# Value projection of token tiles 1 to 7 computed between the steps of an iterative pseudo-inverse and kept in device memory

## The chip, the cores and the metric

The kernel runs on one core of a Trainium2 chip. The metric is the device time of one execution in microseconds (us), and the time of a kernel is the median of its runs. The profile is one further execution of the same program, taken with the hardware profiler. TensorE appears in it as PE (matmuls) and PEld (weight loads), VectorE as DVE, ScalarE as ACT, GpSimd as POOL; SP is the engine that issues most of the plain transfers, in order.

## The reference, cut to what matters

Two layers follow one another. The first is a Nyström attention with a graph gate; its result `xo` replaces the tokens, and a mixture of experts works on these. With `dense` the layer-normed input of 4 x 1024 tokens of width 256, all in float32:

```
attn2_inv = pinv(attn2)            # 6 iterations on 8 matrices of 64 x 64
    xz = x @ z;  z = 0.25 * z @ (13*I - xz @ (15*I - xz @ (7*I - xz)))
xg    = attention of batch 0 (attn1 @ (attn2_inv @ (attn3 @ v)) + conv, output projection)
enc   = xg[0] + dense
A_raw = segment_sum(adj_vals * scores[adj_rows, adj_cols]);  alpha = softmax(A_raw)
value = dense @ wv_w + wv_b        # the value projection of this case: 256 x 256 weights
xl    = alpha[:, None] * value
sw    = sigmoid(-xl) ** 2
xo    = xl * 2 * sw + 2 * enc * (1 - sw)
```

`value` needs only the normed input and two weights. It needs neither the attention nor `alpha`. After this each token goes to expert 0 and to one of seven others (gated silu networks, width 1024).

## The kernel before, in words

The 4096 tokens are cut into 8 token tiles: tile `t` holds tokens 128t to 128t+127 of each of the 4 batches, as `x[t]`, 128 partitions by 4 x 256. All of `x` stays on the chip. The work has these stages:

- 0 to 60 us: inputs, layer-norm statistics `stats[t]` of all tiles (so that a normed tile is one ScalarE pass per batch), `d0T` (the normed batch 0 of all tiles, already transposed), landmarks and weights of the attention.
- 60 to 121 us: the pseudo-inverse. `prod` (L827 to 833) multiplies 8 pairs of 64 x 64 matrices into a PSUM tile; lines 848 to 864 loop over 6 iterations of four such products (`psq`, `pza`, `pzu`, `pzT`; the last iteration has no `pza`), each followed by small VectorE or ScalarE steps (`zu`, `sq`, `zy`, `za`, `zw`, `zT`) on which the next product waits. VectorE works at the same time on the edge lists (`picks`: L253 and L254), and POOL writes the edges to memory with indirect transfers (L276, 73 of them).
- 121 to 187 us: the attention's scores and softmaxes (`score`, `soft`; L917, L926, L934, L947), in pieces. The score tiles use the same two PSUM buffers (`pz`) as the pseudo-inverse.
- 187 to 283 us: output of the attention, the gate `alpha` from the edges, tile 0.
- 283 to 661 us: the dense expert on 8 tiles. The loop issues for each tile `t`: `up(t)` for two of eight column blocks, `down(t-1)`, `prologue(t+1)`, and the other six blocks of `up(t)`. In `up` (L1433) each block takes the PSUM buffers `pa` and `pb` out of four; ScalarE's silu (`sa`, L1444) frees the one, VectorE's product (`h`, L1446) the other.
- 661 to 1063 us: the seven routed experts, in 13 pairs and some single slots of 128 rows.

`prologue(t)` (L1304) normalizes tile `t` (L462), makes its value projection (`turned`, L510: 8 transposes into two PSUM tiles `ptv`, copied to `tv` by VectorE and ScalarE; `values`, L519: 8 products of 128 x 256 with `wv_sb`, and the bias at L534), adds the attention (`added`, L469 and L472), mixes (`mixed`: sigmoid L484, square L488, then L485, L491, L492, statistics, transposes L503), routes the tokens (L1321 to L1354) and writes their slots to memory with POOL (`place`, L1299). `place` reuses its small tile `info` after two tiles, so that VectorE's writes of the next one (L1294) wait for POOL's transfers.

A float32 product shows as two matmul rows and two weight-load rows in the profile, a transpose as one of each.

The order of the work on each engine is made when the program is built: instructions are laid out by expected readiness, per engine, and run in that order. Buffers are taken out of pools in the order of the source. Lines that the change touches: the pseudo-inverse loop (L848 to 864) and lines 1309 to 1312 in `prologue`.

Of the kernel before, what the change touches and what calls it, by code (L numbers as in the profile page):

```python
# [7 lines left out]
F32 = mybir.dt.float32  # L8
BF16 = mybir.dt.bfloat16
I32 = mybir.dt.int32  # L10
AF = mybir.ActivationFunctionType
ALU = mybir.AluOpType
# [4 lines left out]
P = 128  # L17
B, N, D = 4, 1024, 256
NT = N // P
KD = D // P  # L20
# [28 lines left out]
def tile_kernel(  # L49
# [20 lines left out]
    nc = tc.nc  # L70
    mm = nc.tensor.matmul

    def pool(name, bufs=1, **kw):
        return tc.tile_pool(name=name, bufs=bufs, **kw)
# [3 lines left out]
    dram = ctx.enter_context(pool("dram", space=DRAM))  # L78
# [7 lines left out]
    x = [xa[:, t] for t in range(NT)]  # L86
# [26 lines left out]
    ident = const.tile([P, P], F32, name="ident")  # L113
# [47 lines left out]

    meta_d = dram.tile([ROWS, 4], F32, name="meta_d")
    conv_d = dram.tile([H, P * (CW + 1)], F32, name="conv_d")

# [290 lines left out]
    val = [None] * NT  # L457
# [52 lines left out]
    def turned(tt, xt, name, ps, tag, on=None):  # L510

        for k in range(KD):
            pt = ps.tile([P, B, P], F32, tag=tag, name=f"ptv{name}_{k}")
            for b in range(B):
                nc.tensor.transpose(pt[:, b, :], xt[:, b, k * P : (k + 1) * P], ident)
            evac(k if on is None else on, tt[:, k], pt)
        return tt

    def values(t, tt, ps, tag):  # L519

        vt = late.tile([P, B, D], F32, tag="T", name=f"val{t}")
        val[t] = vt
        pvs = []
        for b2 in range(2):
            pv = ps.tile([P, 2, D], F32, tag=tag, name=f"pval{t}_{b2}")
            pvs.append(pv)
            for i in range(2):
                for k in range(KD):
                    mm(pv[:, i, :], lhsT=tt[:, k, 2 * b2 + i, :], rhs=wv_sb[:, k, :],
                       start=(k == 0), stop=(k == KD - 1))  # L530

        def bias():
            for b2 in range(2):
                nc.vector.tensor_tensor(  # L534
                    vt[:, 2 * b2 : 2 * b2 + 2, :], pvs[b2],
                    wvb.unsqueeze(1).to_broadcast([P, 2, D]), ALU.add
                )
        return bias


    with ExitStack() as at:
        wp = at.enter_context(pool("aw"))
        ps = at.enter_context(pool("aps", 4, space=PSUM))
# [14 lines left out]
        for a in a_v:  # L558
            for half in range(2):
                nc.sync.dma_start(  # L560
                    out=a[:, :, half * 512 : half * 512 + 512],
                    in_=zero.unsqueeze(1).to_broadcast([P, NT, 512]),
# [3 lines left out]
        d0T = wp.tile([P, KD, N], F32, name="d0T")  # L566
# [10 lines left out]
        wv_sb = const.tile([P, KD, D], F32, name="wv_sb")  # L577
        nc.sync.dma_start(out=wv_sb, in_=wv_w.rearrange("(k p) d -> p k d", p=P))
        wvb = const.tile([P, D], F32, name="wvb")
# [7 lines left out]
            out=conv_d.rearrange("h (p x) -> p h x", x=CW + 1),  # L587
            in_=zero[:, 0 : CW + 1].unsqueeze(1).to_broadcast([P, H, CW + 1]),
        )
        nc.sync.dma_start(  # L590
            out=conv_d.rearrange("h (p x) -> p h x", x=CW + 1)[:, :, 0:CK],
            in_=conv_rev.unsqueeze(0).to_broadcast([P, H, CK]),
        )
        nc.sync.dma_start(
            out=band, in_=conv_d[:, 0 : P * CW].rearrange("h (p j) -> p h j", j=CW)
# [37 lines left out]
        for i in range(2):  # L633
            wt = ap.tile([P, NP, D], F32, name=f"wT{i}", bufs=1)
            wT.append(wt)
            for h2 in range(2):
                pt = ps.tile([P, 2, D], F32, tag="ps", name=f"ptw{i}_{h2}")
# [13 lines left out]
        stats = [(rstda[:, t], nmra[:, t]) for t in range(NT)]  # L651
        for b in range(B):
# [4 lines left out]
            rstd, nmr = rstda[:, :, b], nmra[:, :, b]  # L657
# [10 lines left out]
            for i, a in ((i, a) for i in range(4) for a in range(2)):  # L668
                t = 4 * a + i
                mm(pool_x[32 * a : 32 * a + 32, b, :], lhsT=gw[:, a, i], rhs=x[t][:, b, :],  # L670
                   start=(i == 0 and b % 2 == 0), stop=(i == 3 and b % 2 == 1))
        for t in range(NT):
            a, i = divmod(t, 4)
            mm(pool_m[32 * a : 32 * a + 32], lhsT=near[:, i], rhs=nmra[:, t, :],
               start=(i == 0), stop=(i == 3))
        for t in range(NT):
# [4 lines left out]
            pt = ps.tile([P, 512], F32, tag="ps", name=f"ptr{t}")[:, 0 : KD * P].rearrange(  # L681
                "p (k n) -> p k n", k=KD
            )
# [7 lines left out]
        pt = ps.tile([P, KD, B, M], F32, tag="ps", name="ptl")  # L691
# [35 lines left out]
        for c in range(NP):  # L727
            pl = ps.tile([P, 2, B * M], F32, tag="ps", name=f"pl{c}")
            for i in range(2):
                f0 = i * H * DH + c * P  # L730
                for k in range(KD):
                    mm(pl[:, i, :], lhsT=wqk8[:, k, f0 : f0 + P],
                       rhs=pT[:, k].rearrange("p b m -> p (b m)"),
                       start=(k == 0), stop=(k == KD - 1))
# [10 lines left out]
        for h2 in range(2):  # L745
            pa2 = ps.tile([P, 8, M], F32, tag="ps", name=f"pa2_{h2}")
            for i in range(8):
                b, c = divmod(h2 * 8 + i, NP)
# [69 lines left out]
        vp = conv.enter_context(pool("v"))  # L818
        inv = ExitStack()
        zp = inv.enter_context(pool("inv", 2))  # L820

        def zt(tag, name):
            return zp.tile([P, NP, M], F32, tag=tag, name=name, bufs=2 if tag in ("za", "zT") else 1)

        def prod(name, lhsT, rhs):  # L827
            pz = psz.tile([P, 2, NP, M], F32, tag="pz", name=name)[:, 0]
            for c in range(NP):
                for j in range(2):  # L830
                    r = slice(64 * j, 64 * j + 64)
                    mm(pz[r, c, :], lhsT=lhsT[r, c, :], rhs=rhs[r, c, :], start=True, stop=True)
            return pz
# [12 lines left out]
        stt = nc.vector.scalar_tensor_tensor  # L846
        for it in range(PINV):
            psq = prod(f"psq{it}", za, za)  # L848
            zu = zt("zu", f"zu{it}")
            stt(zu, za, 7.0, psq, ALU.mult, ALU.subtract)  # L850
            if it < PINV - 1:
                sq = zt("sq", f"sq{it}")
                nc.scalar.activation(sq, psq, AF.Copy, scale=0.25)
                zy = zt("zy", f"zy{it}")
                stt(zy, za, 13.0 / 15.0, psq, ALU.mult, ALU.subtract)
                pza = prod(f"pza{it}", sq, zu)
                zn = zt("za", f"za_{it + 1}")
                stt(zn, zy, 3.75, pza, ALU.mult, ALU.add)
            zw = zt("zw", f"zw{it}")
            stt(zw, za, -15.0, id13.unsqueeze(1).to_broadcast([P, NP, M]), ALU.mult, ALU.add)  # L860
            nc.vector.tensor_tensor(zw, zw, prod(f"pzu{it}", za, zu), ALU.add)
            zTn = zt("zT", f"zT_{it + 1}")
            nc.scalar.activation(zTn, prod(f"pzT{it}", zw, zT), AF.Copy, scale=0.25)
            za, zT = zn, zTn


        tok = const.tile([P, NT * B], F32, name="tok")
# [436 lines left out]
    def prologue(t):  # L1304
        if t:
            def tile_(what):
                return tp.tile([P, B, D], F32, tag=what, name=f"{what}{t}", bufs=2)

            enc = tile_("enc")
            normed(enc, t)  # L1310
            tt = tp.tile([P, KD, B, P], F32, tag="tt", name=f"tv{t}", bufs=1)
            values(t, turned(tt, enc, t, pm, "pm"), pm, "pm")()
            added(enc, t)
            mixed(t, enc, tile_, pm, "pm")
        yt = yT[t]


        pl = pm.tile([P, 512], F32, tag="pm", name=f"plt{t}")
        for k in range(KD):
            for b in range(B):  # L1320
                mm(pl[32 * b : 32 * b + 32, 0:P], lhsT=wr_sb[:, k, :], rhs=yt[:, k, b, :],  # L1321
                   start=(k == 0), stop=(k == KD - 1))
        lg = tp.tile([P, P], F32, tag="lg", name=f"lg{t}", bufs=1)
        nc.scalar.copy(lg, pl[:, 0:P])
        nc.tensor.transpose(pl[:, P : 2 * P], lg, ident)
        plg = pl[:, P : 2 * P].rearrange("p (b e) -> p b e", b=B)[:, :, 0:NX]

        def small(name, w):
            return tp.tile([P, B, w], F32, tag=name, name=f"{name}{t}")

        def bc(a, w):
            return a.to_broadcast([P, B, w])

        mx, sm = small("gmx", 1), small("gsm", 1)
        p, eq, best = small("gp", NX), small("geq", NX - 1), small("gbest", 1)
        den = small("gden", 1)
        nc.vector.tensor_reduce(mx[:, :, 0], plg, AX.X, ALU.max)
        nc.vector.tensor_tensor(p, plg, bc(mx, NX), ALU.subtract)
        nc.scalar.activation(p, p, AF.Exp)
        nc.vector.tensor_reduce(sm[:, :, 0], p, AX.X, ALU.add)  # L1340
        nc.vector.reciprocal(sm, sm)
        nc.vector.tensor_tensor(p, p, bc(sm, NX), ALU.mult)
        nc.vector.tensor_reduce(mx[:, :, 0], p[:, :, 1:NX], AX.X, ALU.max)
        nc.vector.tensor_tensor(eq, p[:, :, 1:NX], bc(mx, NX - 1), ALU.is_equal)
        nc.vector.tensor_tensor(eq, eq, desc.unsqueeze(1).to_broadcast([P, B, NX - 1]), ALU.mult)
        nc.vector.tensor_reduce(best[:, :, 0], eq, AX.X, ALU.max)
        nc.vector.tensor_tensor(eq, eq, bc(best, NX - 1), ALU.is_equal)
        nc.vector.tensor_tensor(den, p[:, :, 0:1], mx, ALU.add)
        nc.vector.tensor_scalar_max(den, den, 1e-9)
        nc.vector.reciprocal(den, den)  # L1350
        nc.vector.tensor_tensor(mx, mx, den, ALU.mult)
        g = main.tile([P, B, 1], F32, tag="gates", name=f"gates{t}")
        gates[t] = g
        nc.vector.tensor_tensor(g, p[:, :, 0:1], den, ALU.mult)  # L1354
        place(t, eq, mx)
# [347 lines left out]
```

## Time and profile before

| what | value |
|---|---|
| runs of the kernel before | 1073.0, 1072.16, 1064.18 us; median 1072.16 us |
| the profiled execution's own time | 1065.04 us |
| its span, first to last instruction | 1063.3 us, mean granted TensorE clock 0.967 |
| busy: PE, PEld, DVE, ACT, POOL | 989.2, 685.7, 437.6, 303.6, 226.2 us |
| stage of the pseudo-inverse, 64.5 to 121.1 us | PE busy 38.4, DVE 29.6, ACT 9.8 of 56.6 us; clock 0.83 |
| one period of the dense expert, 421 to 469 us | PE busy 48.0, DVE 21.9, ACT 20.8 of 48.0 us; clock 1.00 |

How to read it: the busy share of PE over the whole span (93%) mixes a first quarter, in which PE often waits, with the experts, in which it does not. What a change is worth has to be read stage by stage. Busy times count instructions by their modelled ends; for matmuls the distance from one start to the next is the better measure of what one costs.

### The profile page before, as it was taken

Reading aid. Unit: us, or ns where it says so; the run is one execution under the profiler, and the core shown is the slowest. Engines: PE = TensorE matmul, PEld = TensorE weight load, DVE = VectorE, ACT = ScalarE, POOL = GpSimd, SP = SyncE. Lnnn points to the kernel's source line nnn. Section 1 sums busy time; section 2 is a strip of 40 time slices with the busy share of each in tenths; the row PEclk is TensorE's granted clock in tenths of the full one; section 3 lists DMA queues with packets and bytes.
Section 4 is the critical chain, followed back from the end, with each engine's and each line's share of the span. In section 5 each row is a group of like instructions: output and inputs, shape, how many; then the busy total and the mean of one; then the engine's idle time right before and its main releaser. Section 6 shows DMA issues by size and latency. Waiting matters only on the chain. (4 is left out here: it accounts for less than half of the span.)

```text
span 1063.3 us, 13557 instructions
## 1 busy us (share of the span) xinstructions
PE 989.2 (93%) x5042; PEld 685.7 (64%) x5042; DVE 437.6 (41%) x1262; ACT 303.6 (29%) x605; POOL 226.2 (21%) x236
## 2 busy tenths in 40 slices
PE   3867787988999999999999999999999999999996
PEld 2744345564647475756657466888888888866664
DVE  8875477476763544535363621112121211222221
ACT  5321354130661625435171600111101111111111
POOL 1246663003011001010101020332223222322111
PEclk9898897989999999999999999999999999999998
DMA  9810000532300000001010052556545554578880
GB/s 341 290 36 2 1 2 2 218 110 12 140 21 21 20 20 21 20 21 39 1 40 21 21 163 80 178 180 204 206 148 182 208 204 149 189 278 317 297 290 20
DMA packets 74473, 125.30 MB, mean 118 GB/s; under 512 B 11645, under 2 KB 51966, under 8 KB 74400
## 3 DMA queue, kind: packets, MB, share of 16 engines
q1 hardware_dynamic: 63808, 108.50, 29.6%
q0 software_dynamic: 8848, 14.14, 4.5%
q10 hardware_dynamic: 1744, 1.70, 0.5%
q8 instruction: 43, 0.70, 0.3%
q14 instruction: 30, 0.25, 0.1%
HBM read 101.86 MB, written 23.13 MB: 118 GB/s over the span
## 5 line engine op out<-in xcount | busy, mean ns | idle before, releaser
L1441 PE MATMUL pa<-yT,w_a 128*128 128x512 f32 x256 | 124.3, 595 | 0.2 <-issue 0.2
L1441 PE MATMUL pb<-yT,w_a 128*128 128x512 f32 x256 | 122.3, 595 | 0.0
L1453 PE MATMUL po<-w_a,h 128*128 128x256 f32 x512 | 112.3, 379 | 1.1 <-DVE xa L1455 1.1
L1453 PEld LDWEIGHTS po<-w_a,h 128*128 128x128 f32 x512 | 97.1, 190 | 18.5 <-issue 3.8
L1551 DVE TENSOR_TENSOR qh<-qs,qb 128x512 f32<-128x512 f32 x52 | 35.8, 688 | 161.9 <-PE qb L1545 161.9
L1299 POOL DMA_INDIRECT meta_d<-info,pos x32 | 31.4, 980 | 322.6 <-DVE pos L1291 201.8
L1545 PE MATMUL qa<-ypt,w_s 128*128 128x256 f32 x416 | 98.7, 380 | 0.4 <-issue 0.4
L1545 PE MATMUL qb<-ypt,w_s 128*128 128x256 f32 x416 | 98.3, 379 | 0.0
L1549 ACT ACTIVATE qs<-qa 128x512 f32<-128x512 f32 x52 | 31.0, 597 | 224.8 <-PE qa L1545 211.5
L1559 PE MATMUL qo<-w_s,qh 128*128 128x256 f32 x416 | 93.9, 379 | 0.0
L276 POOL DMA_INDIRECT a_d<-pval,cell x73 | 76.5, 1047 | 68.6 <-DMA a_d<-pval,cell 30.7
L1545 PEld LDWEIGHTS qa<-ypt,w_s 128*128 128x128 f32 x416 | 78.0, 190 | 12.6 <-ACT ypt L147 1.1
L1545 PEld LDWEIGHTS qb<-ypt,w_s 128*128 128x128 f32 x416 | 79.0, 190 | 10.7
L1559 PEld LDWEIGHTS qo<-w_s,qh 128*128 128x128 f32 x416 | 78.0, 190 | 10.1
L1441 PEld LDWEIGHTS pb<-yT,w_a 128*128 128x128 f32 x256 | 47.4, 190 | 55.4 <-issue 53.3
L1446 DVE TENSOR_TENSOR h<-sa,pb 128x512 f32<-128x512 f32 x64 | 43.5, 679 | 84.1 <-PE pb L1441 56.9
L1521 POOL DMA_INDIRECT out<-ot,ids x36 | 36.1, 1004 | 196.1 <-DVE ot L1518 179.6
L1441 PEld LDWEIGHTS pa<-yT,w_a 128*128 128x128 f32 x256 | 46.3, 191 | 47.4 <-issue 47.0
L1472 POOL DMA_INDIRECT ys<-y_d,ids x36 | 34.1, 946 | 118.1 <-PE pyp L1531 76.2
L1444 ACT ACTIVATE sa<-pa 128x512 f32<-128x512 f32 x64 | 37.4, 596 | 72.1 <-PE pa L1441 69.0
L1455 DVE SCALAR_TENSOR_TENSOR xa<-po,gates,xa 128x256 f32<-128x256 f32 x32 | 15.3, 483 | 69.2 <-PE po L1453 69.2
L1497 DVE TENSOR_TENSOR sh<-ssa,sb 128x512 f32<-128x512 f32 x20 | 13.8, 688 | 62.6 <-PE sb L1493 62.6
(473 smaller groups left out, 1383.9 us busy)
## 6 DMA issues: line engine op xcount, KB each, us to landing
w_s<-in_w_t SPq DMA_DIRECT2D x69, 1024.0 KB
a_d<-zero SPq DMA_DIRECT2D x4, 2048.0 KB
xa<-in_dense SPq DMA_DIRECT2D x4, 1024.0 KB
av<-a_d SPq DMA_DIRECT2D x8, 512.0 KB
ac<-a_d SPq DMA_DIRECT2D x8, 512.0 KB
y_d<-enc SPq DMA_DIRECT2D x8, 512.0 KB
e_d<-xa SPq DMA_DIRECT2D x8, 512.0 KB
w_a<-in_w_t SPq DMA_DIRECT2D x3, 1024.0 KB
```

Of the source, the lines that this page charges most:

```text
L276: ins = nc.gpsimd.indirect_dma_start(out=a_d[i % PL], out_offset=bass.IndirectOffsetOnAxis(ap=cell[:, i : i + 1], axis=0), in_=pval[:, i : ...
L1299: nc.gpsimd.indirect_dma_start(out=meta_d, out_offset=bass.IndirectOffsetOnAxis(ap=pos[:, b : b + 1], axis=0), in_=info[:, b, :], in_offse ...
L1441: mm(dst, lhsT=w[:, k, f * P : (f + 1) * P], rhs=rhs[:, k, :], start=(k == 0), stop=(k == KD - 1))
L1444: nc.scalar.activation(sa, pa, AF.Silu)
L1446: nc.vector.tensor_tensor(ht, sa, pb, ALU.mult)
L1453: mm(po, lhsT=hs[f][:, b * P : (b + 1) * P], rhs=w2[:, f, :], start=(f == 0), stop=(f == NF - 1))
L1472: nc.gpsimd.indirect_dma_start(out=ys, out_offset=None, in_=src, in_offset=bass.IndirectOffsetOnAxis(ap=ids[:, 0, s : s + 1], axis=0),)
L1521: nc.gpsimd.indirect_dma_start(out=out_rows, out_offset=bass.IndirectOffsetOnAxis(ap=ids[:, 1, s : s + 1], axis=0), in_=ot, in_offset=None ...
L1545: mm(dst[:, i, :], lhsT=wt[:, k, f * P : (f + 1) * P], rhs=yst[:, k].rearrange("p i n -> p (i n)"), start=(k == 0), stop=(k == KD - 1))
L1549: nc.scalar.activation(sa, pa, AF.Silu)
L1551: nc.vector.tensor_tensor(h, sa, pb, ALU.mult)
L1559: mm(po, lhsT=hs[f // 2][:, f % 2, i * P : (i + 1) * P], rhs=w2[:, f, :], start=(f == 0), stop=(f == NF - 1))
```

## The change

Inside the loop of the pseudo-inverse, a generator `fill` is advanced after `psq`, `pza` and `pzu` of each iteration: 17 calls. Its first step prepares a unit, each of the next 14 finishes one unit and prepares the next; the last two calls find nothing left. A unit is half a token tile (two batches). To prepare it, ScalarE normalizes one or two batches again into `fe` (one buffer), PE transposes them into `pft`, ScalarE copies them to `ft`; batch 0 is taken from `d0T` and needs none of this. To finish it, PE makes 4 products into `pfv`, VectorE adds the bias into `fv`, and SP stores 256 KB to `val_d` in memory. In `prologue(t)` for t = 1 to 7 the transposes, copies, products and bias go, and one load of 512 KB from `val_d` into the tile `val` takes their place. The normalization in `prologue` stays, since `enc` is needed there. The `v` projection of the attention (L906) stands in the source behind the loop as before.

```diff
+    val_d = dram.tile([N, B, D], F32, name="val_d")
...
+        fp = inv.enter_context(pool("fill", 2))
+
+        def fill():
+
+            def turn(t, h):
+
+                bs = range(max(2 * h, 1), 2 * h + 2)
+                enc = fp.tile([P, 2, D], F32, tag="fe", name=f"fe{t}_{h}", bufs=1)
+                rstd, nmr = stats[t]
+                for i, b in enumerate(bs):
+                    nc.scalar.activation(
+                        enc[:, i, :], x[t][:, b, :], AF.Identity, bias=nmr[:, b : b + 1],
+                        scale=rstd[:, b : b + 1],
+                    )
+                n = len(bs)
+                pt = ps.tile([P, 2, KD, P], F32, tag="ps", name=f"pft{t}_{h}")
+                for i in range(n):
+                    for k in range(KD):
+                        nc.tensor.transpose(pt[:, i, k, :], enc[:, i, k * P : (k + 1) * P], ident)
+                ft = fp.tile([P, 2, KD, P], F32, tag="ft", name=f"ft{t}_{h}")
+                nc.scalar.copy(ft[:, 0:n], pt[:, 0:n])
+                lhs = [[ft[:, i, k, :] for k in range(KD)] for i in range(n)]
+                if h == 0:
+                    lhs.insert(0, [d0T[:, k, t * P : (t + 1) * P] for k in range(KD)])
+                return lhs
+
+            units = [(t, h) for t in range(1, NT) for h in range(2)]
+            lhs = turn(*units[0])
+            yield
+            for i, (t, h) in enumerate(units):
+                pv = ps.tile([P, 2, D], F32, tag="ps", name=f"pfv{t}_{h}")
+                for j in range(2):
+                    for k in range(KD):
+                        mm(pv[:, j, :], lhsT=lhs[j][k], rhs=wv_sb[:, k, :],
+                           start=(k == 0), stop=(k == KD - 1))
+                vt = fp.tile([P, 2, D], F32, tag="fv", name=f"fv{t}_{h}")
+                nc.vector.tensor_tensor(vt, pv, wvb.unsqueeze(1).to_broadcast([P, 2, D]), ALU.add)
+                nc.sync.dma_start(
+                    out=val_d[t * P : (t + 1) * P, 2 * h : 2 * h + 2, :], in_=vt
+                )
+                if i + 1 < len(units):
+                    lhs = turn(*units[i + 1])
+                yield
+
+        filling = fill()
...
         for it in range(PINV):
             psq = prod(f"psq{it}", za, za)
+            next(filling, None)
...
                 pza = prod(f"pza{it}", sq, zu)
+                next(filling, None)
...
-            nc.vector.tensor_tensor(zw, zw, prod(f"pzu{it}", za, zu), ALU.add)
+            pzu = prod(f"pzu{it}", za, zu)
+            next(filling, None)
+            nc.vector.tensor_tensor(zw, zw, pzu, ALU.add)
...
+        for _ in filling:
+            pass
...
             enc = tile_("enc")
             normed(enc, t)
-            tt = tp.tile([P, KD, B, P], F32, tag="tt", name=f"tv{t}", bufs=1)
-            values(t, turned(tt, enc, t, pm, "pm"), pm, "pm")()
+            val[t] = late.tile([P, B, D], F32, tag="T", name=f"val{t}")
+            nc.sync.dma_start(out=val[t], in_=val_d[t * P : (t + 1) * P])
             added(enc, t)
```

## The prediction

> **What bounds the kernel now.** I read the 40 slices first, then the table of busy time by stage, then PE's timeline and waits in the two stages that the change joins.
>
> ```profile
> PE   3867787988999999999999999999999999999996
> PEclk9898897989999999999999999999999999999998
> ```
>
> From slice 11 (about 283 us) on, PE is busy nine tenths or more. Before that it is not, and the granted clock dips.
>
> ```profile
> core 0: us, PE busy (x) PEld busy (x) DVE busy (x) ACT busy (x) POOL busy (x), PEclk, DMA share, GB/s
> 64.50:121.10 56.60, 38.40 (x422) 21.89 (x421) 29.58 (x126) 9.83 (x21) 34.42 (x36) 0.83 0.02 2
> 421.00:469.00 48.00, 48.00 (x183) 29.94 (x182) 21.87 (x65) 20.82 (x32) 4.00 (x5) 1.00 0.07 23
> ```
>
> The dense expert (second row) is all PE: what PE is spared there comes off the end. In the pseudo-inverse (first row) PE has 18.2 us idle, and a clock of 0.83.
>
> ```profile
> 388.95 1.04 PE L515 MATMUL ptv<-ident,enc 128*128 128x128 f32 x8
> 389.82 1.02 PE L1441 MATMUL pa<-yT,w_a 128*128 128x512 f32 x2
> 390.68 3.62 PE L529 MATMUL pval<-wv_sb,tv 128*128 128x256 f32 x16
> 394.13 1.02 PE L1441 MATMUL pa<-yT,w_a 128*128 128x512 f32 x2
> ```
>
> One tile's value projection, without a gap: from start to next start 0.87 us for 8 transposes (0.109 each) and 3.45 us for 8 products (0.431 each).
>
> ```profile
> 70.03 0.68 PE L832 MATMUL pzu<-zu,za 64*64 64x64 f32 x16
> 70.64 1.12 PE L906 MATMUL pv<-wv,d0T 128*128 128x512 f32 x2
> 76.89 1.12 PE L832 MATMUL pzT<-zT,zw 64*64 64x64 f32 x16 [5.13 <-issue]
> ...
> 98.27 0.63 PE L832 MATMUL psq<-za 64*64 64x64 f32 x16
> 98.84 1.99 PE L906 MATMUL pv<-wv,d0T 128*128 128x512 f32 x4
> 100.75 0.68 PE L832 MATMUL pza<-zu,sq 64*64 64x64 f32 x16
> 101.27 0.63 PE L832 MATMUL pzu<-zu,za 64*64 64x64 f32 x16
> 101.83 1.12 PE L906 MATMUL pv<-wv,d0T 128*128 128x512 f32 x2
> 103.81 0.68 PE L832 MATMUL pzT<-zT,zw 64*64 64x64 f32 x16 [0.86 <-DVE zw L861]
> ```
>
> The stage has already been filled: the attention's `v` projection (L906) stands between the products. Where it fits, an iteration takes 6 us with 0.86 us idle. Elsewhere PE pauses for 5 us.
>
> ```profile
> PE pzT L832 <- issue: 8.5, 2, 5.1
> PE pzT L832 <- DVE zw L861: 6.6, 3, 5.1
> PE pzu L832 <- DVE zu L850: 2.0, 1, 2.0
> PE pza L832 <- ACT sq L853: 1.1, 1, 1.1
> ```
>
> These are all of PE's waits from 64.5 to 121.1 us: 18.2 us, most of it ahead of `pzT`.
>
> **The change part by part.** *Dense expert, removed.* 7 tiles x (0.87 + 3.45) = 30.2 us of PE, at full clock, in a stage without slack: -30.2. VectorE loses 7 copies `tv` (0.69) and 14 bias additions (0.69), ScalarE 7 copies (0.59); both are under half busy, so this counts nothing.
>
> *Dense expert, moved or added.* In the changed kernel's instruction order the mixing of the next tile now runs beside the `up` blocks ahead of `down`, and its transposes stand right behind `down`. ScalarE gets 20 more table loads (68 for 48), 1.28 us each: 26 us over seven periods in which it is busy 20.8 of 48. They stand between the silus, but a silu may be 5 us late before `pa` runs out of buffers (two blocks of 3.44 us), and the densest pair, table loads and a sigmoid between `sa` of blocks 2 and 3, puts it 2.6 us late. Cost 0; without that slack some 2 us a tile. VectorE's wait on POOL moves: the next `info` now stands between `h` of blocks 6 and 7.
>
> ```profile
> 415.56 0.17 DVE L1291 CAST pos<-pf 128x4 int32<-128x4 f32 x1
> 428.15 0.17 DVE L1294 COPY info<-tok 128x4 f32<-128x4 f32 x1 [4.10 <-DMA meta_d<-info,pos]
> ```
>
> From `pos` to the release are 12.6 us here (tile 3), 12.4 at the least (tile 5) and 14.8 at the most (tile 1). Laid out by the rows' durations from the end of `down`, `pos` comes 14.3 us into the new period, so `info` is free at 26.7 to 29.1, and `h` of block 7 follows it; PE needs the `pb` that this frees at 27.9. So 0 to 2.2 us for each of five tiles, most waits at the short end: +1 us (0 to 11).
>
> *The loads of `val`.* 7 x 512 KB on SP's queue, each behind the store `y_d` of an earlier tile and ahead of an `e_d` store; the one of tile 5 is issued some 20 us before ScalarE's sigmoid needs it, the first behind the 3 MB of `w_a` at 268 us and needed about 290. Transfers run at 23 GB/s there, and over 200 GB/s elsewhere in the profile, so 512 KB needs 2.6 us. Cost 0; if a load were exposed in whole, some 3 us a tile.
>
> *Pseudo-inverse, PE.* Full-clock work between the first product (`pxx`) and `score(0)`: before, 24 products of 0.52 (69.51 to 70.03) and 36 rows of 512 columns (`pv`, `p`) of 0.43: 12.5 + 15.5 = 28.0. With 18.2 idle, the remaining 10.4 of 56.6 are what the lower clock costs. After, by the new order: the same products 12.5, `pv` in whole 13.8 (it now mostly follows the loop, with nothing beside it), `p` 2.6, and of the fill's 56 products and 42 transposes (batch 0 needs none) all but 2 and 2, 23.3 + 4.4: together 56.6. So if PE neither waited nor slowed, the stage would be as long as before: the fill takes the whole hole, and the `pv` that covered it is pushed out. What is added is what remains of waits and slow clock. Lower bound 0; upper bound as before, 28.6; a wait of the fill's own can put it above that (rival 4). I take 16: each pause is shortened by one unit of fill (about 2 us: 0.24 to 0.44 of transposes and 1.72 of products), 5.1, 5.1, 3.4, 2.0 becoming 3.1, 3.1, 1.4, 0, in sum 7.6; half of the clock's loss, 5.2; and 0.25 us for each of 14 units in which PE waits for `fe` or `ft`, 3.5. The first of these is the least certain, since two pauses are marked "issue" or "remote", and nothing shown says what they wait for.
>
> The clock by its row is 0.83; at that, the fill's 27.7 us would be 33.4, 6 us more. The Trainium skill (TensorE: Matmul & The Clock Gate, Part 1) has the clock halve after an idle window of about 3.4 us and return after a busy one. By that rule alone, pauses cut to 3.1 us would cost no clock at all, and the sum would be 5 us lower. By that rule, the trace agrees in direction: 1.00 at 97.8 to 103.8 us, without a long pause, and 0.72 at 71.8 to 84.2, around one.
>
> *Pseudo-inverse, others.* ScalarE: 21 normalizations (0.60) and 14 copies (0.38 or 0.59), 19.4 us beside its 9.8 of 56.6: hidden, but with one buffer `fe` the chain transposes, copy, two normalizations is about 2.6 us per unit against 2.9 of PE, so the cover is thin; its price is in the 3.5. VectorE: 14 additions, 9.7 us beside 29.6. They delay `picks`; POOL's transfer 33 needs them at 104.2 where they were done at 89.3, transfer 49 at 128.9 for 101.6, so 15 us of slack hide it. SP: 14 stores of 256 KB, on a queue that waits from 55 to 186 us for nothing but POOL's last transfer:
>
> ```profile
> SPq L1025 <- DMA a_d<-pval,cell: 125.8, 1, 125.8
> ```
>
> That last transfer waits for VectorE (L333, 10.3 us idle on POOL) late in the attention, so a longer pseudo-inverse delays everything behind it in full.
>
> Sum: -30.2 + 1 + 16 = -13.2. Against the profiled execution, 1065.04, that is 1051.8; its span is 1063.3, and the 1.7 us around it stay. The profiled run lies 7.1 us below the median of the runs shown, 1072.16; two of three are at 1072 to 1073. On the median: 1059.
>
> **The rivals.**
>
> 1. *The hole swallows all:* waits and slow clock shrink to 0 to 7 us, PE's queue being full. For it: iterations with enough filling wait 0.86 us of 6. Against: the long pauses came in spite of `pv` in the queue. -30.2 + 1 + 4 = -25: 1047.
>
> 2. *The gain is given back:* the pauses belong to PE or to its supply and not to missing work, so they and the slow clock stay, 25 to 32 us. For it: 8.5 us of waits with no releaser, and the same "issue" gaps in `pb` (L970) later, on POOL's busy stretch. -30.2 + 1 + 28.6 = -0.6: 1071.6. Here a large removal shows as no change.
>
> 3. *The stall moves to VectorE in the dense expert:* `info` costs its 2.2 us, and a table load as much, per tile: +11 + 14 on top of 16 gives +11: 1083, but the slack of two blocks has to fail for both; I count it within the chances of 4.
>
> 4. *Slower: the fill runs at half clock.* If PE waits for ScalarE's chain at each unit, it is idle often enough that the clock stays down. 56.6 us of work at the 0.60 that 165.9 to 187 us had is 94.3, with 7.6 of pauses +45: net +16, 1088. It decides for slower by over 1% once the stage grows by over 40 us, which is a mean clock under 0.65 with those pauses. Against it: at 97.8 to 103.8 us, filled, the clock was 1.00.
>
> **How the numbers follow.** A difference under about 1% (10.7 us) is what a measurement of this kernel can't tell from no change. My forecast, a stage longer by 9 to 24 us and so 1052 to 1067, has 0.50; rival 1, 1041 to 1052, 0.17; rival 2, 1067 to 1075, 0.20; rival 4 with 3, 0.13. Faster by over 1% is below 1061.4: all of rival 1 and two thirds of the forecast, 0.50. Within 1%: the rest of the forecast and nearly all of rival 2, 0.36. Slower: 0.14. The range 1044 to 1076 leaves out about half of rival 1 and rival 4.
>
> **What would show it.** In the changed kernel's profile: a period of the dense expert of 43.7 us for 48 (right) or over 45 (rival 3), with VectorE's wait at L1294 in front of `h`; no PE wait on a `val` load. `score(0)` about 16 us later than 121 us; at 121 rival 1, past 146 rival 2, with pauses ahead of `pzT` still at 5 us; past 161 with a clock under 0.65 rival 4. `pv` as an unbroken block of about 12 us behind the loop. From `score(0)` to 283 us the stages should keep their lengths; if they shrink or grow by more than 3 us, the forecast has missed something that was shared. It is wrong altogether if the dense expert doesn't lose 30 us.

## The result, and the profile after

| | runs | median (lowest to highest) |
|---|---|---|
| before | 20 | 1071.03 us (1059.15 to 1082.74) |
| after | 20 | 1060.97 us (1050.43 to 1073.98) |

The ratio is 0.9896, 95% interval 0.9872 to 0.9919: faster by 1.0%. It is taken over the fast runs alone: runs over 1.5% above the fastest of the same kernel are left out of it, but not out of the medians. The profiled execution of the changed kernel took 1056.15 us (span 1054.4), 8.9 us under that of before. The forecast was 1059, or 0.988 of the median of 1072.16 that was known before. The time is close to the forecast; the way there is not.

PE in 40 slices after the change: it is nearly full from slice 11 on as before, and fuller ahead of it. Before the last slice, three digits of the clock are under 9, all after 184 us (slices 7, 9 and 10, counted from 0). Before the change there were five, between 26 and 240 us.

```profile
PE   3888799898999899999999999999999999999996
PEclk9999999896899999999999999999999999999998
```

Busy time by stage, after: the pseudo-inverse, the attention up to its output, and one period of the dense expert.

```profile
core 0: us, PE busy (x) PEld busy (x) DVE busy (x) ACT busy (x) POOL busy (x), PEclk, DMA share, GB/s
64.60:148.10 83.50, 69.79 (x571) 47.39 (x571) 38.37 (x138) 25.13 (x54) 49.59 (x53) 0.94 0.14 45
148.10:202.80 54.70, 47.88 (x538) 28.52 (x536) 44.09 (x105) 32.49 (x152) 17.63 (x14) 0.94 0.02 3
430.57:474.28 43.71, 43.71 (x158) 25.86 (x157) 20.20 (x63) 24.39 (x34) 3.83 (x4) 1.00 0.12 37
```

The dense expert's period is 43.7 us where it was 48.0, and PE is busy all through it. The pseudo-inverse has grown from 56.6 to 83.5 us, 11 more than forecast. But the attention behind it, which the change does not touch, has shrunk. This is its row before:

```profile
121.10:187.30 66.20, 55.41 (x538) 32.38 (x536) 44.44 (x104) 32.47 (x152) 33.52 (x30) 0.84 0.02 3
```

The same 538 matmuls took 66.2 us at a clock of 0.84 and now take 54.7 at 0.94. One group of products shows how. Before, the 32 small products of `pb` came in a beat of 0.71 to 0.75 us, with pauses marked "issue":

```profile
134.90 0.96 PE L970 MATMUL pb<-v,e3T 128*64 128x64 f32 x21
136.28 0.34 PE L970 MATMUL pb<-v,e3T 128*64 128x64 f32 x3 [0.41 <-issue]
137.00 0.28 PE L970 MATMUL pb<-v,e3T 128*64 128x64 f32 x2 [0.38 <-issue]
137.75 0.31 PE L970 MATMUL pb<-v,e3T 128*64 128x64 f32 x3 [0.47 <-issue]
138.49 0.26 PE L970 MATMUL pb<-v,e3T 128*64 128x64 f32 x1 [0.44 <-issue]
139.20 0.29 PE L970 MATMUL pb<-v,e3T 128*64 128x64 f32 x2 [0.46 <-issue]
```

After, the same group is one row:

```profile
160.91 1.15 PE L1022 MATMUL pb<-v,e3T 128*64 128x64 f32 x32
```

These are PE's waits in the longer pseudo-inverse, after, in sum 13.6 us. In this profile the 5 us pauses ahead of `pzT` are gone; others stand in other places, and four of the rows are marked "issue".

```profile
PE pza L878 <- ACT sq L900: 5.0, 2, 3.5
PE pzu L878 <- DVE zu L897: 2.7, 1, 2.7
PE pfv L855 <- issue: 1.8, 6, 0.4
PE psq L878 <- issue: 1.4, 2, 1.1
PE pzT L878 <- DVE zw L911: 1.2, 1, 1.2
PE pfv L855 <- ACT ft L842: 0.9, 3, 0.4
PE pft L840 <- issue: 0.3, 1, 0.3
PE pzu L878 <- issue: 0.3, 1, 0.3
```

From the first `pa` to the end of the last `po` the dense expert took 381.2 us before and takes 356.2: 25.0 less, not 30. The rest is lost in the first two periods, whose largest wait is this one (VectorE, then PE, after):

```profile
355.97 0.17 DVE L1346 COPY info<-tok 128x4 f32<-128x4 f32 x1 [7.04 <-DMA meta_d<-info,pos]
...
356.58 0.68 DVE L151 COPY yT<-pty 128x512 f32<-128x512 f32 x1
```

```profile
357.32 0.64 PE L1373 MATMUL plt<-yT,wr_sb 128*32 128x128 f32 x16 [3.73 <-DVE yT L151]
357.89 1.30 PE L1493 MATMUL pa<-yT,w_a 128*128 128x512 f32 x2
358.99 0.42 PE L1377 MATMUL plt<-ident,lg 128*128 128x128 f32 x1
359.20 3.34 PE L1493 MATMUL pb<-yT,w_a 128*128 128x512 f32 x4
```

VectorE stood 7.0 us before it could write `info`, with the copy `yT` queued behind it, on which PE's `plt` waits; the row of four `pb` matmuls after the pause took 3.34 us where such a row takes 1.88, and the granted clock from 355 to 363 us was 0.79. That period is 49.0 us, the later ones 43.7. In the period before, `h` came late behind the same wait, and PE lost 1.8 us there.

**Stages of all runs.** The columns are distances in us between the starts of the first `pxx` (the pseudo-inverse), of `score(0)`, of the attention's output `po` and of the dense expert's first `pa`, then to the end of the dense expert's last `po`, all read from PE's timelines. What follows (the routed experts) is 398 to 402 us in every run.

| run | `pxx` to `score(0)` | to `po` | to first `pa` | to last dense `po` | span |
|---|---|---|---|---|---|
| before | 56.6 | 66.3 | 95.4 | 381.2 | 1063.3 |
| after | 83.5 | 54.7 | 95.6 | 356.2 | 1054.4 |
| e1 fill only | 61.3 | 52.7 | 93.5 | 382.5 | 1055.4 |
| e2 loads only | 32.0 | 54.1 | 107.2 | 356.1 | 1014.9 |
| e3 before, no scatters | 32.0 | 52.6 | 92.1 | 384.1 | 1026.3 |
| e4 after, no scatters | 61.3 | 52.7 | 92.9 | 353.4 | 1028.1 |
| e5 before again | 61.5 | 68.7 | 94.9 | 383.9 | 1074.5 |
| e6 after again | 93.0 | 55.3 | 93.3 | 358.5 | 1064.0 |
| e7 `info` 8 | 81.3 | 57.3 | 95.7 | 348.9 | 1049.3 |
| e8 three tiles | 72.5 | 65.7 | 95.7 | 373.2 | 1071.6 |
| e9 before, `info` 8 | 32.0 | 54.2 | 104.1 | 378.4 | 1034.4 |
| e10 before, no scatters | 32.0 | 54.1 | 94.1 | 385.2 | 1031.3 |
| e11 fill behind the loop | 32.2 | 81.1 | 93.9 | 356.2 | 1026.8 |
| e12 spread, `info` 8 | 41.0 | 74.7 | 108.7 | 348.9 | 1039.2 |

Three sets of four ran on three chips: e1 to e4, e5 to e8, e9 to e12. On the first and the third the unchanged kernel took 1039.08 and 1042.78 us (medians of 7 and 20), on the second 1070.28, as in the comparison above. Each ratio is to the kernel before on the same chip. The unchanged kernel before was profiled in the comparison above and as e5, the changed one in the comparison and as e6. On the first and the third chip the stages without a fill are read from e2, e3, e9 and e10.

### The profile page after: what moved, and what is told of

It reads as the page before. It is cut to its first block, busy times and chain, and to the rows that moved or that the text cites. A ratio compares the mean times of both kernels' runs of the same rounds, so it can differ in the third digit from the quotient of the medians.

```text
span 1054.4 us, 13619 instructions
## 1 busy us (share of the span) xinstructions
PE 988.6 (94%) x5028; PEld 684.4 (65%) x5028; DVE 431.0 (41%) x1255; ACT 343.6 (33%) x653; POOL 224.7 (21%) x236
## 5 line engine op out<-in xcount | busy, mean ns | idle before, releaser
L1611 PE MATMUL qo<-w_s,qh 128*128 128x256 f32 x416 | 93.9, 379 | 0.0
L1597 PEld LDWEIGHTS qb<-ypt,w_s 128*128 128x128 f32 x416 | 79.0, 190 | 10.7
L1549 DVE TENSOR_TENSOR sh<-ssa,sb 128x512 f32<-128x512 f32 x20 | 13.7, 687 | 62.6 <-PE sb L1545 62.6
```

What stands on the lines that cost most here:

```text
L1597: mm(dst[:, i, :], lhsT=wt[:, k, f * P : (f + 1) * P], rhs=yst[:, k].rearrange("p i n -> p (i n)"), start=(k == 0), stop=(k == KD - 1))
L1611: mm(po, lhsT=hs[f // 2][:, f % 2, i * P : (i + 1) * P], rhs=w2[:, f, :], start=(f == 0), stop=(f == NF - 1))
```

## The experiments

**e1, the fill alone.** The changed kernel, with the removed lines put back into `prologue`:

```diff
-            val[t] = late.tile([P, B, D], F32, tag="T", name=f"val{t}")
-            nc.sync.dma_start(out=val[t], in_=val_d[t * P : (t + 1) * P])
+            tt = tp.tile([P, KD, B, P], F32, tag="tt", name=f"tv{t}", bufs=1)
+            values(t, turned(tt, enc, t, pm, "pm"), pm, "pm")()
```

> The changed kernel with the fill and its stores kept, but with every tile's value projection made again in the dense expert, as before (what the fill stores is not read). It prices the fill alone. If the two halves of the change add up, the stages up to the first pa are those of the changed kernel (score(0) at about 148 us, first pa at about 298) and the dense expert those of the kernel before (period 48.0 us): first pa 15.6 us later than before and nothing given back, so 1.4 to 1.5% slower than before. If the shorter attention (11 us) hung on something in the dense expert or on the loads, first pa would come at about 309 us, 2.5% slower.

**e2, the removal and the loads alone.** The changed kernel with an empty fill and another source for `val`, so that the value projection of tiles 1 to 7 is left out:

```diff
-        filling = fill()
+        filling = iter(())
...
-            nc.sync.dma_start(out=val[t], in_=val_d[t * P : (t + 1) * P])
+            nc.sync.dma_start(out=val[t], in_=dense_v[:, t])
```

> The changed kernel without the fill: the value projection of tiles 1 to 7 is left out, and as val each tile loads rows of the input of the same size, at the same place in the queue. It prices the removal and the loads alone. As predicted, the dense expert gives 30.2 - 1 = 29 us, first pa stays at 283 us: 2.7% faster than before. If the stalls seen in the changed kernel (1.8 us in the first period and some 5 in the second, on the release of info) belong to the shorter prologue and the loads, they are here too: 24 to 25 us, 2.3% faster, and the waits stand in the first two periods.

Measured: e1 1.0175 (1.0144 to 1.0206), e2 0.9798 (0.9775 to 0.9822). The time of e1 is where the first view had it. That of e2 is outside both views, and the stages behind the two times are others than expected. These are windows of e2 (the pseudo-inverse, then from `po` to the first `pa`):

```profile
65.90:97.90 32.00, 31.16 (x420) 18.17 (x420) 29.10 (x127) 9.97 (x21) 18.53 (x20) 1.00 0.02 2
152.10:259.30 107.20, 91.71 (x691) 59.55 (x692) 60.67 (x132) 25.50 (x45) 25.39 (x27) 0.82 0.39 123
```

And the same windows of e1:

```profile
65.90:127.20 61.30, 61.30 (x572) 44.12 (x572) 38.26 (x138) 24.96 (x54) 36.65 (x38) 1.00 0.18 62
179.90:273.40 93.50, 83.75 (x692) 55.29 (x692) 60.27 (x132) 25.94 (x46) 8.43 (x10) 0.91 0.44 135
```

On this chip there is no hole in the pseudo-inverse: without the fill PE is busy 31.2 of 32.0 us at full clock. The fill adds 29.3 us, or 2.09 for each of 14 units, which is about what it removes later.

The hole is behind the attention. There PE counts the cells that the edges have filled (`cnt`), from marks that VectorE makes (`nz`) of the cells loaded back from memory, and those loads wait for POOL's last scatter. In e2 that scatter was issued at 177.4 us, and PE had come to the end of its other work by 178 us:

```profile
177.40 0.97 POOL L277 DMA_INDIRECT a_d<-pval,cell  x1 [1.92 <-DMA a_d<-pval,cell]
183.32 0.69 DVE L1079 TENSOR_SCALAR nz<-av 128x1024 bf16<-128x1024 f32 x1 [24.13 <-DMA av<-a_d]
184.07 0.37 PE L1083 MATMUL cnt<-onesb,nz 128*128 128x1 bf16 x8 [6.20 <-DVE nz L1079]
```

All of PE's waits at `cnt`, in e2 and then in e1, where PE comes to the count later:

```profile
PE cnt L1083 <- DVE nz L1079: 9.3, 5, 6.2
PE cnt L1083 <- DVE nz L1079: 2.4, 3, 1.4
```

From `po` to the first `pa` e2 takes 107.2 us and e1 93.5. The waits are 6.9 of this difference of 13.7; the mean clock is 0.82 in the one and 0.91 in the other. In e2 the stalls of the first two periods are there too (3.0 and 2.1 us), without any fill: they belong to the shorter prologue and the loads.

**e3 and e4, no scatters.** In both kernels POOL's 72 scatters of the picked edges are left out; a limit is raised so that the branch for rows to be redone is not taken:

```diff
         value(pval[:, cs], [s[:, cs] for s in packed], b)
-        scatter(range(cs.start, cs.stop))
...
-            if i and i % REST == 0:
+            if scattered and i % REST == 0:
...
-        nc.vector.tensor_scalar(worst, worst, float(EG), 0.0, ALU.subtract, ALU.max)
+        nc.vector.tensor_scalar(worst, worst, float(1 << 20), 0.0, ALU.subtract, ALU.max)
```

> The kernel before without POOL's 72 scatters of the picked edges (the adjacency's cells are left out, the last scatter stays, and the count of rows to be redone is held at zero so that no branch is taken); VectorE's picks stay. Only the stages up to po are read. Theory 1 (PE's pauses marked issue, and the slow matmuls around them, belong to the stretch in which POOL issues scatters, until 168 us): the 8.5 us ahead of pzT and the 5.7 us in pb go, the pseudo-inverse stage falls from 56.6 to 40 to 46 us and the attention from 66 to about 55. Theory 2 (they belong to PE, to its clock after idle time, or to missing work): both stages keep their lengths within 3 us.

> The changed kernel without the same 72 scatters. Theory 1: the pseudo-inverse stage, 83.5 us, loses the pauses at 85 to 88, 99 to 103 and 111 to 119 us and the late releases: 65 to 72 us; the attention, of which all but 20 us lies behind the scatters already, stays at 54.7 within 2. Theory 2: 83.5 us within 3.

Measured: 1028.05 and 1029.9 us, one run each. The pauses are absent on this chip with scatters too (e1, e2), so the runs say nothing on theory 1. They say what the wait for the scatters is worth: without it the stage from `po` to `pa` takes 92.1 us, where e2 took 107.2. The same pair on the third chip is 94.1 (e10) and 104.1 (e9). With that wait gone the change gains nothing: the fill adds 30.2 us up to the first `pa` (206.9 for 176.7), the dense expert gives 30.7 back, and the span is 1.8 us longer.

**e5 and e6, both kernels unchanged,** on the second chip.

> The kernel before, unchanged, profiled on the chip of these runs. In the last set the stage from pxx to score(0) took 32.0 us without the fill, with or without POOL's scatters, and 61.3 with it, and the kernel before took 1039 us for 1071. If the pauses marked issue are the chip's or the placement's and not the program's, this kernel shows here either 56 us with pauses (time about 1070) or 32 us without (about 1039), and nothing between; without them PE comes to the counting of cells (cnt) ahead of POOL's last scatter and waits 9 to 13 us for it, where e2 waited 9.3. If the pauses are the program's, they are here at any time of the kernel.

> The changed kernel, unchanged, beside it. Theory (the fill is serial PE work of 2.09 us for each of 14 units, 29.3 us, and the cover is the wait for POOL's last scatter behind the attention): without pauses score(0) comes 29.3 us later, first pa 15 to 18 later, since 11 to 13 of it are wait, and the dense expert gives 25 back: 7 to 10 us faster, ratio 0.990 to 0.993. Rival (holes in the pseudo-inverse are what pays): without holes nothing pays, and the time is that of before or 4 us above (30.2 removed, 29.3 added, 5 of stalls).

Measured: e5 1076.24 us (one run), with pauses; e6 0.9949 (0.99 to 0.9998). The pseudo-inverse that takes 32 us without a fill on two chips takes 61.5 here. What was expected of e6 was worked out for a chip without pauses, so it is not tested. The change adds 31.5 us to that stage, and the attention gives 13.4 back: the two sides of the pair above (26.9 and 11.6) are there again. The pauses ahead of `pzT` are not gone in e6, though its kernel is the changed one: their longest are 4.4 and 4.1 us. In all six profiles with pauses (before, after, e5 to e8) PE's waits marked "issue" end at 172 us or earlier; from there to 260 us they sum to 0.2 us at most.

**e7, eight buffers for `info`** in the changed kernel:

```diff
-        info = tp.tile([P, B, 4], F32, tag="info", name=f"info{t}", bufs=2)
+        info = tp.tile([P, B, 4], F32, tag="info", name=f"info{t}", bufs=8)
```

> The changed kernel with 8 buffers for info in place of 2, so that VectorE no longer waits for POOL's transfers of two tiles earlier. If the stalls of the first two periods (1.8 us in pb, 3.7 us ahead of plt and 1.5 of slow matmuls behind it) hang on that release: both gone, 6 to 7 us faster than the changed kernel. If POOL's transfers are late because the stores and loads of 512 KB collide with them, and something else needs them, the waits only move: within 2 us.

Measured: 0.9811 (0.9763 to 0.9859). The dense expert takes 348.9 us (after: 356.2; e6: 358.5). These are all of PE's waits from 298 to 660 us, first in the changed kernel (after), then in e7:

```profile
PE plt L1373 <- DVE yT L151: 3.7, 1, 3.7
PE pb L1493 <- DVE h L1498: 1.8, 1, 1.8
PE qa L1597 <- issue: 0.4, 1, 0.4
PE pa L1493 <- issue: 0.2, 1, 0.2
```

```profile
PE qa L1597 <- issue: 0.4, 1, 0.4
PE plt L1373 <- ACT yT L147: 0.3, 1, 0.3
PE pa L1493 <- issue: 0.2, 1, 0.2
```

POOL's transfers of the second routed tile are as late as ever (the last issued at 353.75 us; 352.74 in the changed kernel), but nothing waits for them. So what was lost in the first two periods was lost to the release of `info`, and not to the transfers' own pace. This version is faster than both kernels, and its interval does not touch that of e6. Its time is some 15 us below that of e6, more than the 7.3 to 9.6 that the dense expert gives: the pseudo-inverse was 81.3 us in its profile for 93.0 in that of e6, with the same code in that stage, so that part is not shown to be the edit's.

**e8, three tiles.** The changed kernel with `range(1, 4)` in place of `range(1, NT)` in `units`, and the value projection of tiles 4 to 7 in `prologue` as before.

> Tiles 1 to 3 alone are filled and loaded, tiles 4 to 7 are projected in the dense expert as before. Theory (serial fill, covered only by the wait for the scatters): 6 units add 12.5 us to the pseudo-inverse, all but 0 to 3 of it covered, and 13.0 less stalls of 2 to 5 come off the dense expert: as fast as the changed kernel within 3 us; tiles 4 to 7 pay nothing there. Rival (every tile pays alike): 3/7 of the changed kernel's gain.

Measured: 0.9992 (0.9944 to 1.004). The interval overlaps with that of e6, and 3/7 of e6's gain lies inside it as well, so the time does not decide. The stages say more. The pseudo-inverse is 11.0 us longer than in e5 for 6 units, and the attention gives only 3.0 back, so that 8.8 us reach the first `pa`: the expected cover of all but 0 to 3 us was not there. The dense expert takes 373.2 us, 8.0 less than before and 10.7 less than e5 on the same chip, where 3 x 4.32 = 13.0 were removed. The two stalls are there in full (1.9 and 3.8 us): three tiles pay the stall of seven.

**e9, eight buffers for `info` in the kernel before.**

> The kernel before with 8 buffers for info, as in e7. There PE's own waits in the dense expert are 2.0 us, and VectorE's waits on info (27 us) stand where PE has work queued: 0 to 2 us faster than before. If it is as much as in the changed kernel (7 to 10 us in the dense expert there), the gain of e7 is not the change's to claim but any version's.

Measured: 0.9956 (0.9935 to 0.9977), or 2.4 to 6.8 us faster, more than expected. The dense expert takes 378.4 us, 2.8 below before, and PE's waits of 2.0 us in it are gone. So the buffers are worth some 3 to 5 us in the kernel before, and 7 to 10 in the dense expert of the changed one.

**e10, e3 once more.**

> e3 again: the kernel before without the 72 scatters, on whatever chip this set gets. On a chip on which the kernel before takes 1065 us or more, and so has pauses: theory 1 (the pauses belong to the stretch of POOL's scatters, 64 to 172 us in all five profiles that have them): no waits marked issue, pxx to score(0) 32 to 35 us, attention 52 to 55. Theory 2 (they come with the chip whatever POOL does): 55 to 62 us and 60 to 69. On a chip on which it takes about 1039 us it tells nothing new.

The third chip has no pauses either: e10 takes 1033.1 us (one run) for 1042.78, with the stages within 2 us of e3's. Whether the pauses of the other chips need POOL's scatters stays untested.

**e11, the fill written behind the loop:** the three `next(filling, None)` taken out, the draining `for _ in filling` left as it is.

> The changed kernel with the whole fill behind the pseudo-inverse's loop and none between its steps. If placing the units between the steps absorbs waits, as predicted, score(0) comes 5 to 12 us later than in the changed kernel and the time is that much longer. If PE's loss is a matter of the stretch of time up to 170 us, and not of missing work, the order within it does not matter: the changed kernel's time within 3 us (ratio to before 0.988 to 0.998 on a chip with pauses).

Measured, on the third chip: 0.9878 (0.9851 to 0.9905), about the change's ratio in the comparison above (0.9896); the change as it stands was not run on this chip. The program's layout still put some of the units between the products of the loop, and the rest between the first `p` of the attention, so this is another order and not the absence of one. From `pxx` to `po` it takes 113.3 us, and e1 114.0: the order does not matter where PE has no hole. What it does on a chip with pauses, for which the expectation was written, is not tested.

**e12, the fill spread,** with `info` as in e7: one unit for each iteration of the loop, the rest one by one ahead of `pzb`, `po`, two counts, `ptab`, `par`, `pg_bad` and `ptot`; ScalarE evacuates and stores the units.

> e7 (8 buffers for info) with the fill spread: 5 units between the steps of the pseudo-inverse, one per iteration, and 9 later, each ahead of a wait of PE between the end of the attention and the dense expert (ahead of pzb, po, two of the counts, ptab, par, pg_bad, ptot); ScalarE evacuates and stores, and the bias is added when the tile is loaded. If those waits (11 us in all, none over 2.4) and the slow clock there take up half of the 18.8 us moved: 5 to 10 us faster than e7, ratio 0.972 to 0.977. If an attention that starts 19 us sooner falls back into the stretch with pauses, or the units stand on the path there in full: e7's 0.981 within 0.004, or slower.

Measured: 1.0012 (0.9999 to 1.0026). The dense expert has e7's 348.9 us, but from `pxx` to the first `pa` it takes 224.4 us, where e11 on the same chip takes 207.2. This is PE from 165 us on:

```profile
165.51 0.38 PE L840 MATMUL pft<-ident,fe 128*128 128x128 f32 x2
181.29 0.24 PE L1081 MATMUL cnt<-onesb,nz 128*128 128x1 bf16 x3 [15.40 <-DVE nz L1077]
181.39 0.67 PE L840 MATMUL pft<-ident,fe 128*128 128x128 f32 x2
181.85 0.32 PE L1081 MATMUL cnt<-onesb,nz 128*128 128x1 bf16 x5
182.03 2.05 PE L1045 MATMUL po<-a1T,xbd 128*128 128x512 f32 x2
```

The new layout put the first count ahead of `po`. PE came to it 15.4 us before the first cells were there (they are loaded behind the last scatter), with 20 us of work on `po` behind it in its queue. The wait took the place of the cover.

## Why the time was right and the path was not

**Dense expert, -30.2: right in size.** The period is 43.71 us for the 43.7 foretold. No PE wait is on a `val` load, and the table loads are hidden (ScalarE is busy 24.4 of 43.7 us).

**`info`, +1: mis-sized.** PE lost 1.8 us in the first period, at the place foretold, and 5.3 in the second (49.0 less 43.7). Before, it had lost 2.0 itself in the dense expert. So 30.2 - 1.8 - 5.3 + 2.0 = 25.1 us come off, and 25.0 were measured. By the prediction's own sign ("if the dense expert doesn't lose 30 us") that is a miss: 5.1 us for the 1 foretold. It lay inside the bounds of 0 to 11, but it was laid out for a settled period. The later periods cost nothing; in the second one VectorE's wait stands ahead of `yT` and not between two `h`. e7 shows that the release alone was the price.

**Pseudo-inverse, +16: the step that failed.** It said that of 28.6 us of pauses and slow clock 16 would be left, because filled pauses shrink. The chips without pauses give the bare stage: 32.0 us without the fill (estimated 28.0), 61.3 with it (estimated 56.6). So 4 of the 10.4 us that the prediction put down to the clock were work. Against the bare stage the loss was 56.6 - 32.0 = 24.6 us before and 83.5 - 61.3 = 22.2 after; on the second chip it was 29.5 before (e5), and 31.7 and 20.0 with the same fill (e6, e7). Filling removed nothing that is clear of this spread. The stage came out 10.9 us longer than forecast: 4.7 of it is work and 6.2 is loss that did not shrink. The pauses were not missing work, as rival 2 held. Of its two markers `score(0)` past 146 us came true at 148.1; pauses of about 5 us ahead of `pzT` were not there after, but were in e6 (4.4) and e7 (5.7). The clock did rise, from 0.83 to 0.94. By the rule of the idle window in the Trainium skill (TensorE: Matmul & The Clock Gate, Part 1), taken alone, pauses under about 3.4 us cost no clock. Here it was 0.79 from 88 to 96 us, with no wait over 1.14 us in the 8 us ahead, so that rule does not account for this row.

**"A longer pseudo-inverse delays everything behind it in full": the second step that failed, the other way.** Of 26.9 us only 15.6 reached the first `pa`. On the chips without pauses the cover is the wait for POOL's last scatter with the slow clock beside it, 10 to 14 us; e3 and e4 show it by taking it away, and with it the gain. On the chips with pauses the cover is the attention, which before had 12.3 us of loss (66.3 against 54) while it lay at 121 to 187 us and after has 2 at most at 148 to 203. In e8 it lay at 137 to 203 us and gave back only 3.0. That the pauses end with POOL's stretch of scatters (the last of the dense row at 168 us in both kernels) is what the times agree on; it is not shown that the scatters make them, and what does is open.

So two errors of about 11 us cancelled: the stage grew by 10.9 us more than foretold, and the attention gave 11.6 back of which nothing was foretold. The net of 15.6 met the 16 by luck. The two profiles are 8.9 us apart where 13.2 was forecast, mainly by the 4.1 us too little for `info`. The text's own test ("if they shrink or grow by more than 3 us, the forecast has missed something that was shared") points at the stage in which it was missed.

**Costed at nothing, and right:** `pv` stands as an unbroken block behind the loop (13.07 us), and POOL's scatters are not late (the last but one was issued at 168.30 us for 167.48).

## What to carry to other kernels

Work that is moved out of a stage bound by PE into another one bound by PE gains nothing by itself (30.7 us given back for 30.2 added, in e3 and e4). Look for something that runs at a pace of its own, like a long run of transfers, and ask whether the moved work fits ahead of the wait for it. Before reading a stage's idle time as room, see on another chip or in another run whether it is the program's. When a step gets shorter, look at the small buffers that a slow transfer releases: six more copies of a tile of 64 bytes per partition took 7 to 10 us out of the changed kernel's dense expert, where the whole change had gained 5 to 11.

## What the runs showed of the hardware

The same kernel takes 1039 and 1043 us on two chips, 1070 on a third, and 1071 in the comparison above. By the stages the difference lies between 64 and 172 us: where the kernel takes 1070 us, PE pauses there, marked "issue" or behind results that come late, and its clock dips. Against the chips without pauses, before and e5 lose 24.6 and 29.5 us in the pseudo-inverse and 12 to 15 in the attention, less the 9 to 12 us by which the others are longer from `po` to the first `pa`. In `pb` before, after such pauses, PE issued in steps of 0.71 to 0.75 us. The pauses are not PE's alone: in before, after, e7 and e8 ScalarE too has a wait of 1.2 to 3.1 us ahead of `sq` that is marked "issue", and in none of the eight profiles of the other two chips. The other stages of the kernel before agree within 4 us. Each set ran on one chip, so the runs do not tell whether it is the chip itself or where the program lay on it.
